# Moving two of each step's score-maximum chunks into the score tile, in a four-layer attention and FFN kernel

## Chip, core and metric

The kernel runs on one core of one Trainium2 chip. The metric is the device time of one execution in microseconds. Three runs of the kernel before gave 11,102.46, 11,116.24 and 11,129.85 us, a median of 11,116.24.

## The reference

A batch of 16 sequences x of 256 tokens and 128 channels goes through four layers. Each layer adds an attention result and then a feed-forward result (experts, convolution or plain) to x. Every layer has a cross attention of 16 heads over a context of 1,601 positions with 64 channels. In layers l0, l1 and l3 a head has 8 channels, in l2 it has 32; l0 and l2 also attend over the 256 tokens themselves. The part that the change touches is the softmax of the cross attention:

```
scores = jnp.einsum('bhqd,bhkd->bhqk', qh, kh) * scale
attn = jax.nn.softmax(scores, axis=-1)
out = jnp.einsum('bhqk,bhkd->bhqd', attn, vh)
```

The softmax is taken with its row maximum subtracted, so for each head and each of the 256 queries the kernel needs the largest of 1,601 scores before it can form the first exponential.

## The kernel before

**Slabs and steps.** The cross attention of one sequence in one layer is cut into four slabs of four heads; 16 sequences, four layers and four slabs make 256 slabs, two sequences being in flight. The heads of a slab stand in four groups of 32 partitions. For the 8-channel heads the 32 rows hold high and low parts of queries and keys, in a rounded fp32 format (`spread`, L407 ff.); in l2 they hold 32 channels in fp32. A slab's main loop has seven steps (`Slab.steps`, L530): six take two key tiles of 128, the last takes the remaining 65 keys.

**One step of the main loop** (L1169 to L1192) issues, in this order:

1. `maxima(part - 3)`: some chunks of the *next* slab's row maxima;
2. `st_ops` (L447): the scores of this slab, transposed, keys on partitions. Two score tiles of two PSUM banks each, `sc[0]` for heads 0 and 1, `sc[1]` for heads 2 and 3. The products go key tile by key tile over the four heads, and then one product per head adds the negated row maximum (`nmT`);
3. `exps` (L462): one ScalarE exponential for each score tile, PSUM to SBUF;
4. `maxima(part)`: three more chunks of the next slab;
5. `weigh_back` (L1132): the value products of the *previous* step, accumulated in one PSUM bank `av` that is held over the slab (in l2 also products with ones, for the sums);
6. two or three calls of `slot` (L1073), which advance all side work by one piece each: keys, values and contexts of later slabs, the layers' projections, norms and feed-forward parts.

Under the manual schedule each engine executes its instructions in this written order, so an instruction that waits holds up all that is behind it on its engine.

**Maxima chunks.** A slab needs 32 of them: two query halves q, four chunks c of about 400 keys, four heads g, queued in `self.todo` with g innermost (L537 ff.). `Slab.maxima` (L544) takes the first of the queue: one product of 128 queries by 400 keys into a PSUM bank (`bank`, tile group `pb`, four banks), and one VectorE `tensor_reduce` (L552) of this bank into `mx[:, q, g, c]`. Two closures are returned; the loop helper `maxima(want)` issues the products at once and the reductions after them. With `part = 32 * (j + 1) // 6` the six full steps take 5, 5, 6, 5, 5 and 6 chunks, three of them after the scores. In the seventh step `thirds` (L556) reduces `mx` to the negated maximum (L558), GpSimd splits it into three bf16 parts, and `shift` transposes them to `nmT` for the next slab.

**PSUM.** Eight banks: tile group `ps` has two score tiles of two banks (tag `st`), group `pb` four single banks. One of these holds `av`; the other three serve the maxima chunks and all side work. The tiles of the self attention (`own_attention`, L564, in slots of l0 and l2) use the two score tiles too.

Of the kernel before, what the change touches and what calls it, by code (L numbers as in the profile page):

```python
# [11 lines left out]
F32 = mybir.dt.float32  # L12
# [4 lines left out]
ALU = mybir.AluOpType  # L17
AX = mybir.AxisListType
PSUM = bass.MemoryType.PSUM

P = 128
T = 256
# [32 lines left out]
def rows_of(kt):  # L55
    return min(P, NK - kt * P)
# [18 lines left out]
def model(ctx: ExitStack, tc: tile.TileContext, d, out):  # L75
    nc = tc.nc
# [78 lines left out]
    ps = ctx.enter_context(tc.tile_pool(name="ps", bufs=2, space=PSUM))  # L155
# [4 lines left out]
    def name(base):  # L160
        uid[0] += 1
        return f"{base}_{uid[0]}"

    def bank():
        return pb.tile([P, 512], F32, tag="bank", name=name("bank"))
# [5 lines left out]
    def mm(o, l, r, start=True, stop=True, free=False):  # L171
        nc.tensor.matmul(out=o, lhsT=l, rhs=r, start=start, stop=stop, skip_group_check=free)  # L172
# [6 lines left out]
    with setup as sp:  # L179
# [24 lines left out]
        p = bank()  # L204
# [11 lines left out]
        p = bank()  # L216
# [230 lines left out]
    def st_ops(att, s, t0, n, r, nmT, pairs=(0, 1)):  # L447


        sc = {hp: ps.tile([P, 2, 2, T], F32, tag="st", name=name("st")) for hp in pairs}  # L450
        heads = [g for hp in pairs for g in (2 * hp, 2 * hp + 1)]
        for i in range(n):
            k0 = (t0 + i) * P
            for g in heads:
                h = slice(32 * g, 32 * g + 32)
                mm(sc[g // 2][:r, g % 2, i, :], att.k[s][h, k0 : k0 + r], att.q[h, s, :], i == 0, False)
        for g in heads:
            h = slice(32 * g, 32 * g + 32)
            mm(sc[g // 2][:r, g % 2, :n, :], ones16[h, :r], nmT[h, :].unsqueeze(1).broadcast_to([32, n, T]), False, True)
        return [sc[hp] for hp in pairs]  # L460

    def exps(att, sc, n, r):  # L462
        e = probs()
        nc.scalar.activation(e[:r, :, :n, :], sc[:r, :, :n, :], AF.Exp, scale=att.scale)  # L464
        return e

    def zeroed(att):
        a = bank().rearrange("p (u q) -> p u q", u=2)
        n = 1 if att.d8 else 2
        mm(a[:, :n, :], zero16[:, :P], zero16.unsqueeze(1).broadcast_to([1, n, T]), True, False, True)  # L470
        return a

    def weigh(att, s, av, pr, t0, n, r, last, heads=range(4), sums=True, values=True):
        for i in range(n):
            fin = last and i == n - 1
            if values:
                for g in heads:
                    m = 9 if att.d8 else 32
                    mm(av[32 * g : 32 * g + m, 0, :], att.value(s, t0 + i, g, r), pr[g // 2][:r, g % 2, i, :],
                       False, fin, True)  # L480
            if sums and not att.d8:
                for g in heads:
                    mm(av[32 * g : 32 * g + 32, 1, :], ones[:r, :32], pr[g // 2][:r, g % 2, i, :], False, fin, True)
# [21 lines left out]
    def thirds(n, nm):  # L505

        r = sm.tile([P, 2, 4], F32, tag="third", name=name("third"))
        a, b, c = (n[:, :, i::32] for i in range(3))
        nc.gpsimd.tensor_copy(a, nm)  # L509
        nc.gpsimd.tensor_tensor(r, nm, a, ALU.subtract)  # L510
        nc.gpsimd.tensor_copy(b, r)
        nc.gpsimd.tensor_tensor(c, r, b, ALU.subtract)
# [14 lines left out]
    class Slab:  # L527


        steps = [(t, min(2, NT - t), rows_of(t)) for t in range(0, NT, 2)]  # L530
# [13 lines left out]
        def maxima(self):  # L544

            g, q, c, k0, k1 = self.todo.popleft()
            att, s = self.att, self.s
            p = bank()
            h = slice(32 * g, 32 * g + 32)

            def reduce():
                nc.vector.tensor_reduce(self.mx[:, q, g, c : c + 1], p[:, : k1 - k0], AX.X, ALU.max)  # L552

            return lambda: mm(p[:, : k1 - k0], att.q[h, s, q * P : (q + 1) * P], att.k[s][h, k0:k1]), reduce

        def thirds(self):  # L556
            nm = sm.tile([P, 2, 4], F32, tag="nm", name=name("nm"))
# [498 lines left out]
    def advance(g):  # L1056
        try:
            return True, next(g)
        except StopIteration:
            return False, None  # L1060
# [12 lines left out]
    def slot():  # L1073
        begin()
        if later:
            g = later.popleft()
            if advance(g)[0]:
                later.appendleft(g)
        for i, l in enumerate(lines):
            if i == turn[0] % 2:  # L1080
                advance(l)
        turn[0] += 1
        for c in list(chains):
            if c[0] is not None and c[0] in ready:
                if not ready[c[0]].done:
                    continue
                del ready[c[0]]
            alive, att = advance(c[1])
            if att is not None:
                ready[c[0]] = att  # L1090
            if not alive:
                chains.remove(c)

    def until(cond):
        for _ in range(2000):
            if cond():
                return
            slot()
        raise RuntimeError("the slots do not come to an end")
# [3 lines left out]
    def slab(i):  # L1103

        n, s = divmod(i, 4)
        if n >= len(seq):
            return None
        b = seq[n][0]
        until(lambda: b in ready and not ready[b].done and n in k_of and s in k_of[n])
        att = ready[b]  # L1110
        att.k, att.v = k_of[n], v_of.setdefault(n, {})
        slabs_of[i] = Slab(att, s, i % 2)
        return slabs_of[i]

    def finish(sl, i):

        yield from normalised(sl.att, sl.s, sl.av)
        if sl.s == 3:
            sl.att.done = True
        if not sl.att.d8 or sl.s == 3:  # L1120
            vp_room.give()

    with tc.manual_schedule():
        sl = slab(0)
        while sl.todo:
            for o in sl.maxima():
                o()
        sl.thirds()
        sl.shift()
        back = None  # L1130

        def weigh_back():  # L1132

            nonlocal back
            if back is None:
                return
            sl, i, j, pr = back
            n = i // 4
            t0, m, r = sl.steps[j]
            if j == 0:  # L1140
                until(lambda: (0 if sl.att.d8 else sl.s) in v_of.get(n, {}))
                sl.att.v = v_of[n]
                sl.av = zeroed(sl.att)
            last = j == len(sl.steps) - 1
            weigh(sl.att, sl.s, sl.av, pr, t0, m, r, last)
            back = None
            if last:
                g = finish(sl, i)
                if advance(g)[0]:
                    later.append(g)  # L1150

        for i in range(4 * len(seq)):
            nxt = slab(i + 1)
            steps = sl.steps
            emitted = 0

            def maxima(want):

                nonlocal emitted
                ops = []  # L1160
                while nxt is not None and emitted < want:
                    a, c = nxt.maxima()
                    a()
                    ops.append(c)
                    emitted += 1
                for c in ops:
                    c()

            for j, (t0, m, r) in enumerate(steps):  # L1169

                part = 32 * (j + 1) // (len(steps) - 1)
                if j < len(steps) - 1:
                    maxima(part - 3)
                elif nxt is not None:
                    nxt.thirds()
                sc = st_ops(sl.att, sl.s, t0, m, r, sl.nmT)
                pr = [exps(sl.att, t, m, r) for t in sc]
                if j < len(steps) - 1:
                    maxima(part)
                weigh_back()  # L1180
                back = (sl, i, j, pr)
                if j == len(steps) - 1 and nxt is not None:
                    nxt.shift()
                slot()
                slot()

                if i // 4 + 1 < len(seq) and seq[i // 4 + 1][1] == "l2":
                    slot()
            kp_room.give()
            sl = nxt  # L1190
        weigh_back()
        until(lambda: not chains and not later)  # L1192
# [119 lines left out]
```

## Time and profile before

| | |
|---|---|
| median of three runs | 11,116.24 us |
| the profiled execution's time | 11,069.08 us |
| its span, first to last instruction | 11,067.1 us |
| mean granted TensorE clock | 0.815 of full speed |
| TensorE products busy | 9,761.1 us (88%) |
| VectorE busy | 5,929.3 us (54%) |
| ScalarE busy | 4,978.5 us (45%) |
| single maxima, L552 | 8,192, 4,155.2 us busy |
| exponentials, L464 | 3,840, 3,500.5 us busy |
| chunk products (`bank<-k,q`) | 3,573.1 us busy |

PE is TensorE's products, PEld its weight loads, DVE VectorE, ACT ScalarE, POOL GpSimd, SP the queue that issues most transfers. Busy times of a group are the union of its instructions, so pipelined instructions count once; the mean of one is its own latency. All TensorE products are recorded by one helper, L172, and are told apart by the tiles they write and read: `bank<-k,q` a maxima chunk, `st<-q,k` a score product, `bank<-p,v` a value product. An fp32 product stands in the trace twice. A group's line ends with its engine's idle time just before it and with what ended that idle time.

### The profile page before, as it was taken

The page shows a single profiled execution, that of the slowest core. Times are in us where ns is not written, and L with a number is a line of the kernel's source. Part 1 is how long each engine was busy: PE and PEld are TensorE (multiplying, and loading weights), DVE is VectorE, ACT ScalarE, POOL GpSimd, SP SyncE. Part 2 cuts the span into 40 slices and gives each one's busy share as a digit, 9 for nine tenths or more (in the row PEclk, how much of TensorE's full clock was granted, in tenths as well). Part 3 has the DMA queues.
Part 4 walks back from the last instruction along what each step waited for, and adds up shares of the span by engine and source line. Part 5 has one row for each costly group of instructions (what it writes and reads, how often), then busy time and mean ns, then how long its engine had stood idle before and what let it go on. Part 6 is the DMA issues. An engine that isn't in the chain of part 4 may idle for free.

```text
span 11067.1 us, 204917 instructions
## 1 busy us (share of the span) xinstructions
PE 9761.1 (88%) x86834; PEld 5294.4 (48%) x86874; DVE 5929.3 (54%) x13070; ACT 4978.5 (45%) x6812; POOL 952.3 (9%) x2283
## 2 busy tenths in 40 slices
PE   6989899897998979889798897998979889898898
PEld 3445444454444544445454454444545445444454
DVE  5545555455554555545455454554555545465455
ACT  3544455444553445434454344543445434454444
POOL 2000100001000010000100001000010000100000
PEclk8779777797878978789777897778977789687898
DMA  2100111001110011100111001110011100111011
GB/s 58 37 7 15 36 45 37 7 16 39 42 37 7 19 38 42 34 7 19 38 44 32 7 19 42 40 32 7 19 38 43 33 7 19 38 44 32 7 24 27
DMA packets 158828, 313.10 MB, mean 28 GB/s; under 512 B 65163, under 2 KB 116275, under 8 KB 157910
## 3 DMA queue, kind: packets, MB, share of 16 engines
q1 hardware_dynamic: 154676, 297.83, 11.7%
q8 instruction: 683, 11.19, 0.4%
q14 instruction: 235, 1.93, 0.1%
q0 software_dynamic: 768, 1.48, 0.0%
q10 hardware_dynamic: 2466, 0.68, 0.0%
HBM read 98.31 MB, written 2.10 MB: 9 GB/s over the span
## 4 chain that ended last, share of the span: by engine, by line
PE 71%; DVE 14%; ACT 5%; issue 4%; POOL 3%; SPq 2%; DMA 1%; another core or an unknown queue 0%; DVEq 0%; POOLq 0%; ACTq 0%
PE bank L172 57%; PE st L172 10%; DVE mx L552 5%; ACT p L464 3%; DVE nm L579 2%; SPq L411 2%; PE mx L172 1%; PE bank L492 1%; POOL p L603 1%; PE bank L298 1%; DVE z L282 1%; POOL rs L278 1%; DVE st L275 1%; DVE hl L405 1%; ACT y L239 1%
## 5 line engine op out<-in xcount | busy, mean ns | idle before, releaser
L552 DVE TENSOR_REDUCE mx<-bank 128x1 f32<-128x400 f32 (+2 forms) x8192 | 4155.2, 567 | 2296.9 <-PE bank L172 2271.8
L464 ACT ACTIVATE p<-st 128x1024 f32<-128x1024 f32 (+1 forms) x3840 | 3500.5, 963 | 3568.3 <-PE st L172 2358.6
L172 PE MATMUL bank<-k,q 32*128 32x400 f32 (+2 forms) x10240 | 3573.1, 557 | 495.3 <-DVE mx L552 261.3
L172 PEld LDWEIGHTS bank<-k,q 32*128 32x128 f32 x10240 | 1600.6, 211 | 1928.7 <-DVE mx L552 1111.4
L172 PE MATMUL bank<-p,v 128*9 128x256 f32 (+3 forms) x27648 | 2412.4, 460 | 12.6 <-POOL p L603 12.6
L172 PE MATMUL st<-q,k 32*128 32x256 f32 (+1 forms) x18176 | 1974.8, 391 | 126.2 <-DVE nm L579 69.2
L172 PEld LDWEIGHTS st<-q,k 32*128 32x128 f32 (+1 forms) x18176 | 1300.8, 210 | 443.7 <-ACT p L464 140.4
L172 PE MATMUL st<-nmT,ones 32*128 32x512 bf16 (+1 forms) x7680 | 1270.1, 435 | 0.0
L172 PEld LDWEIGHTS bank<-p,v 128*9 128x9 f32 (+3 forms) x27648 | 676.3, 104 | 1175.4 <-issue 922.6
L172 PE MATMUL bank<-p,ones 128*32 128x256 f32 (+1 forms) x7680 | 607.1, 389 | 18.1 <-ACT p L464 18.1
L509 POOL CAST nmp<-nm 128x8 bf16<-128x8 f32 x384 | 83.6, 218 | 5441.9 <-DVE nm L558 3668.7
L278 POOL TENSOR_TENSOR rs<-rs,neghalf 128x2 f32<-128x2 f32 x240 | 167.5, 698 | 3491.1 <-DVE rs L277 3491.1
L172 PEld LDWEIGHTS <-ones 32*128 32x128 bf16 (+1 forms) x7680 | 408.1, 108 | 39.4
L579 DVE TENSOR_REDUCE nm<-mx 128x4 f32<-128x1024 f32 x256 | 301.8, 1221 | 215.3 <-PE mx L172 210.6
L239 ACT COPY v<-bank 128x512 f32<-128x512 f32 (+3 forms) x592 | 228.6, 448 | 328.8 <-PE bank L172 328.8
L172 PEld LDWEIGHTS bank<-p,ones 128*32 128x32 f32 (+1 forms) x7680 | 250.8, 113 | 216.6 <-ACT p L464 43.6
L502 DVE RECIPROCAL rc<-bank 128x256 f32<-128x256 f32 x128 | 224.9, 1757 | 193.6 <-PE bank L172 189.3
L603 POOL TENSOR_SCALAR_AFFINE_SELECT p<-p 128x1024 f32<-128x1024 f32 x256 | 266.6, 1063 | 653.3 <-PE bank L172 352.7
L464 ACT ACT_TABLE_LOAD x141 | 180.9, 1283 | 312.9 <-PE st L172 201.9
L172 PE MATMUL bank<-ws,h 128*128 128x128 f32 x1664 | 297.9, 343 | 3.2 <-DVE h L1027 0.8
L768 DVE TENSOR_TENSOR x<-bank,x 128x256 f32<-128x256 f32 x144 | 61.1, 425 | 446.0 <-PE bank L172 446.0
L172 PEld LDWEIGHTS bank<-ws,h 128*128 128x128 f32 x1664 | 267.2, 248 | 39.0 <-DVE mx L552 13.6
(240 smaller groups left out, 7274.4 us busy)
## 6 DMA issues: line engine op xcount, KB each, us to landing
k<-hl SPq DMA_DIRECT2D x768, 200.2 KB, 4.0
q<-hl SPq DMA_DIRECT2D x1024, 32.0 KB, 1.9
ws<-in_s_l_a_li_dram SPq DMA_DIRECT2D x32, 768.0 KB, 4.3
ws<-in_s_l3f_dram SPq DMA_DIRECT2D x32, 768.0 KB, 6.7
ws<-in_s_l0f_dram SPq DMA_DIRECT2D x32, 512.0 KB, 5.6
ws<-in_s_l_a_qkv_dram SPq DMA_DIRECT2D x16, 768.0 KB
k<-hl SPq DMA_DIRECT2D x256, 32.0 KB, 1.9
ws<-in_s_l3f_dram SPq DMA_DIRECT2D x16, 384.0 KB
```

The costliest lines, as they stand in the source:

```text
L172: nc.tensor.matmul(out=o, lhsT=l, rhs=r, start=start, stop=stop, skip_group_check=free)
L239: nc.scalar.copy(o, i)
L275: nc.vector.bn_stats(out=st[:, q, :], in_=src[:, q, :])
L278: nc.gpsimd.tensor_tensor(rs, rs, neghalf[:, 0:2], ALU.pow)
L282: nc.vector.tensor_scalar(z[:, q, :], src[:, q, :], mv[:, q, 0:1], rs[:, q : q + 1], ALU.subtract, ALU.mult)
L298: nc.tensor.transpose(p[:, q * P : (q + 1) * P], z[:, q, :], ident)
L411: nc.sync.dma_start(out=raw(o)[r::4, :], in_=raw(hl[c])[32 * s : 32 * s + 32, :])
L464: nc.scalar.activation(e[:r, :, :n, :], sc[:r, :, :n, :], AF.Exp, scale=att.scale)
L502: nc.vector.reciprocal(rc, av[:, 1, :])
L552: nc.vector.tensor_reduce(self.mx[:, q, g, c : c + 1], p[:, : k1 - k0], AX.X, ALU.max)
L579: nc.vector.tensor_reduce(o, sc[hp], AX.X, ALU.max, negate=True)
L603: nc.gpsimd.affine_select(out=e, in_=e, pattern=[[0, 2], [sign * P, 2], [-sign, T]], compare_op=op, fill=0.0, base=0, channel_multiplier=sign,
```

## The change

A new method takes two chunks from the other end of the queue (the last of the list: two neighbouring heads of one q and c), writes their products into the two banks of a *score tile* (group `ps`, tag `st`) instead of two single banks, and reduces both with one instruction of 128 x 2 x 400 elements, whose output is two elements per partition. It is called once in each of the six full steps, after the value products of `weigh_back` and before the slots. The tile that is free first at this point is the one that the step's first exponential reads. The other 20 chunks are taken as before, in the new shares 3, 3, 4, 3, 3 and 4 per step, of which two (not three) stand after the scores.

```diff
+        def maxima2(self):
+
+            q, c, k0, k1 = self.todo.pop()[1:]
+            g0 = self.todo.pop()[0]
+            p = ps.tile([P, 2, 2 * T], F32, tag="st", name=name("mx2"))
+            for g in (g0, g0 + 1):
+                h = slice(32 * g, 32 * g + 32)
+                mm(p[:, g - g0, : k1 - k0], self.att.q[h, self.s, q * P : (q + 1) * P], self.att.k[self.s][h, k0:k1])
+            nc.vector.tensor_reduce(self.mx[:, q, g0 : g0 + 2, c], p[:, :, : k1 - k0], AX.X, ALU.max)
...
-                part = 32 * (j + 1) // (len(steps) - 1)
+
+                part = (32 - 2 * (len(steps) - 1)) * (j + 1) // (len(steps) - 1)
                 if j < len(steps) - 1:
-                    maxima(part - 3)
+                    maxima(part - 2)
                 elif nxt is not None:
                     nxt.thirds()
                 sc = st_ops(sl.att, sl.s, t0, m, r, sl.nmT)
...
                 back = (sl, i, j, pr)
+                if j < len(steps) - 1 and nxt is not None:
+                    nxt.maxima2()
                 if j == len(steps) - 1 and nxt is not None:
                     nxt.shift()
                 slot()
```

## The prediction

> **What bounds the kernel now.** I read the page first (busy shares, chain of waits, costliest groups), then the table of waits, then the timeline.
>
> ```profile
> PE 9761.1 (88%) x86834; PEld 5294.4 (48%) x86874; DVE 5929.3 (54%) x13070; ACT 4978.5 (45%) x6812; POOL 952.3 (9%) x2283
> ...
> PE 71%; DVE 14%; ACT 5%; issue 4%; POOL 3%; SPq 2%; DMA 1%; another core or an unknown queue 0%; DVEq 0%; POOLq 0%; ACTq 0%
> ...
> L552 DVE TENSOR_REDUCE mx<-bank 128x1 f32<-128x400 f32 (+2 forms) x8192 | 4155.2, 567 | 2296.9 <-PE bank L172 2271.8
> L172 PEld LDWEIGHTS bank<-k,q 32*128 32x128 f32 x10240 | 1600.6, 211 | 1928.7 <-DVE mx L552 1111.4
> L579 DVE TENSOR_REDUCE nm<-mx 128x4 f32<-128x1024 f32 x256 | 301.8, 1221 | 215.3 <-PE mx L172 210.6
> ```
>
> PE carries the chain. VectorE is half idle, and yet the weight loads of the chunk products wait 1,111 us for its maxima. The table of waits says the same:
>
> ```profile
> PEld bank L172 <- DVE mx L552: 1304.6, 3116, 5.7
> PEld st L172 <- ACT p L464: 140.4, 215, 1.8
> ```
>
> Score tiles hardly wait for the exponentials (140 us); banks wait for maxima. Where that sits is seen in a step that has nothing else on PE (timeline; start, length, engine):
>
> ```profile
> 3011.38 0.45 PE L172 MATMUL bank<-k,q 32*128 32x400 f32 x2
> 3011.38 0.56 PE L172 MATMUL st<-q,k 32*128 32x256 f32 x6
> ...
> 3011.86 2.50 DVE L552 TENSOR_REDUCE mx<-bank 128x1 f32<-128x400 f32 x5 [0.98 <-PE bank L172]
> ...
> 3012.39 1.94 ACT L464 ACTIVATE p<-st 128x1024 f32<-128x1024 f32 x2 [1.13 <-PE bank L172]
> 3012.49 0.18 PEld L172 LDWEIGHTS bank<-k,q 32*128 32x128 f32 x1 [0.49 <-DVE mx L552]
> ...
> 3013.34 1.05 PE L172 MATMUL bank<-p,v 128*9 128x256 f32 x16
> ```
>
> Two chunk products, the scores, a third chunk; then all three free banks are full (the fourth holds the running sum), and chunks four and five go at VectorE's 0.5 us rhythm. The value products start 1.96 us after the scores. And a step with other work:
>
> ```profile
> 3030.87 0.56 PE L172 MATMUL st<-q,k 32*128 32x256 f32 x7
> ...
> 3031.53 0.60 DVE L282 TENSOR_SCALAR z<-x,mv,rs 128x128 f32<-128x128 f32 x2 [0.82 <-POOL rs L278]
> 3031.88 1.94 ACT L464 ACTIVATE p<-st 128x1024 f32<-128x1024 f32 x2 [1.07 <-PE st L172]
> 3032.05 2.97 DVE L552 TENSOR_REDUCE mx<-bank 128x1 f32<-128x400 f32 x6
> 3032.68 1.41 PE L172 MATMUL bank<-k,q 32*128 32x400 f32 x3 [0.90 <-DVE mx L552]
> ...
> 3034.01 1.05 PE L172 MATMUL bank<-p,v 128*9 128x256 f32 x16
> ```
>
> A layer norm holds VectorE, so all six maxima come late and the value products start 3.14 us after the scores.
>
> **What the Trainium skill says.** "Perfetto Trace Analysis", Identifying Performance Opportunities: the same gap repeating on the engine that should be saturated can mean too little PSUM for the next tile. The trace agrees (0.3 to 0.5 us at each late chunk). "VectorE: DVE Perf Modes", The perf-mode tier table: a reduction runs at 1x only, so width costs in full. It agrees: (1221-567) ns for 624 more elements is 1.05 ns each. "TensorE: Matmul & The Clock Gate", Part 1: TensorE runs at half clock unless recent windows were busy. It agrees: the mean grant is 0.815, and a chunk product takes 0.41 us in some steps and 0.70 in others.
>
> **The steps counted.** I cut the timeline at each step's first chunk product (steps j = 0 to 4 of each slab, 1,275 in all; times 6/5 for j = 5) and sorted by the length from the last value product to the next chunk product; under 0.7 us I call a step bare. "Period" is first exponential to first exponential; "b-w" first score product to first value product.
> - bare, 8-wide heads, full clock: 172 (206 scaled), period 3.17, b-w 2.24
> - bare, 8-wide, half clock: 145 (174), 4.37, 2.34
> - bare, layer l2: 104 (125), 4.62, 2.87
> - with side work: full clock 388 (466), b-w 2.16; half 250 (300), 2.92; l2 216 (259), 3.20
>
> **Part 1, chunks taken out of the b-w stretch.** 3 or 4 bank chunks remain of 5 or 6 in each of six steps, with two after the scores instead of three. With three banks free nothing waits for a maximum of its own step. What remains of b-w at full clock: the scores' products (0.75 us at 3014.42) plus the last chunk's 0.37 to the value products, about 1.15 us (the step at 3024.99, whose chunks did not wait, took 1.21 to the clearing product ahead of its value products). At half clock 1.5, by the same sum from 3007.65; in l2, where each score product stands twice in the trace, 2.1 (2.10 from the first score to the first exponential). So PE saves 1.0, 1.4 and 1.1 us, less the moved pair's own products: 0.1 (two row groups side by side; three in a row start within 0.1 at 3014.33), 0.2 and 0.3.
>
> **Part 2, the pair's wait for the first exponential.** It ends 1.97 us after the scores start (1.01 + 0.97 in the bare step), while value products that start at 1.15 are through at 2.1; at half clock 2.64 against 3.3, in l2 3.07 against 4.0. Hidden by the value products: 0. Where a table load or an evacuation delays the exponential, PE and all side work behind it wait; in PE's queue these are the two slots' products.
>
> **Part 3, one reduction for two chunks.** No row has 800 elements; between the rows for 400 and 1024: 567 + 400 x 1.05 = 0.98 us. Bounds: 0.92 (two at the 0.507 spacing of 4155.2/8192, one fixed part less) to 1.2 (the 1024 row). VectorE's total falls by at most 0.1 x 1,530 = 150 us; it is 54% busy, so nothing. Behind it stand the slots' VectorE operations. Today their place is behind the last maximum, which ends 3.0 to 3.4 us after the scores start (14.36 in the bare step); in the new order the pair ends at 3.6. These 0.2 to 0.6 us are taken off what passes to the next step, below.
>
> **Part 4, the score tile held.** This is the new wait. The next step's first two heads take the second exponential's tile; heads three and four need the pair's. In a bare step at full clock: pair products at b+2.1, first maximum 0.48 later (the 3011.38 row to the 3011.86 row), 0.98 for the reduction, 0.04 to PE: b+3.6. From there 0.9 to the next exponential (1.01, less the two products already made): b+4.5, a period of 3.5 against 3.17. Half clock: 3.3+0.74+0.98+0.04+1.45-1.67 = 4.84 against 4.37. l2: 4.0+0.97+0.98+0.04+1.9-2.1 = 5.8 at most, 5.7 taken, against 4.62. Loss: 206 x 0.33 + 174 x 0.47 + 125 x 1.08 = 68+82+135 = **+285 us**. With over about 1.5 us of side work on PE this wait is covered.
>
> **The sum.** Side-work steps could save 466 x 0.9 + 300 x 1.2 + 259 x 0.8 = 419+360+207 = 986 us if all of it reached the next step. It doesn't: in two thirds of them PE already waits over 0.3 us inside the slots for ScalarE or VectorE (transposes that wait for an evacuation, products that wait for a layer norm), and these engines are no earlier, since the second exponential still ends 2.94 us after the scores start. I let a third pass in full and a quarter of the rest: 0.34 + 0.66/4 = 0.5, so 493 us. Bounds: 0.15 (only where PE never waits, less what banks take) to 0.8. Net 285-493 = -208, about **-200 us**. The profiled execution spans 11,067.1 us and took 11,069.08, so 10,869; it is 47 us under the median 11,116.24 of the three runs, on which the forecast is 10,916.
>
> No DMA is moved. The last step's pair delays the slab's negated maximum (L558), but the score tile that the next step needs is freed by the same reduction, so the shift is no later against the scores.
>
> **Rivals.**
> - *The score tile becomes the bound (slower).* Place: third and fourth head of each next step's scores. For it: bare steps are a third of all, and the side-work slots are short in many others (1.3 us typical for one class in each layer). Against it: VectorE is free when the pair arrives. It decides once less than 285/986 = 0.29 of the saving passes. At 0.1: +285-99 = +186, 11,302 us. TensorE at half clock more often, because it waits more, pulls the same way.
> - *All passes (much faster).* In the layer-norm step above, the late maxima cost two steps' worth, which my sum doesn't credit. At 0.95: 285-937 = -652, 10,464 us. Against it: PE's waits for ScalarE in the slots.
> - *Cancelled.* 0.29 passes: about 11,116.
> - *It doesn't do what it says:* the pair may be given the second exponential's tile. It would then wait until b+3.0, nearly 1 us more in every step; I count it with the slower case.
>
> **Chances.** Forecast case, -35 to -480 us: 0.42. All passes: 0.12. Within 0.3% (33 us; about what a measurement can tell from no change): 0.10. Slower: 0.36. So faster 0.54. Range: 0.8 passing gives -504; 0.15 gives +137: 10,612 to 11,253, taken as 10,620 to 11,250, with about one in ten left out at each end.
>
> **What would show it.** Right: the waits of PE for L552's single maxima fall from 1,566 us (1304.6 + 261.3) below 500; b-w near 1.2 in full-clock steps; a new wait "PE st <- DVE mx2" of 300 to 800 us, in bare steps; bare periods of 3.5, 4.8 and 5.7; VectorE busy within 3% of before. Wrong: that wait over 1,000 us, or spread over steps with side work; the pair's products waiting over 300 us for the exponential; a mean grant below 0.79.

## The result, and the profile after

The changed kernel is slower: 11,542.98 us (median of four runs, 11,527.76 to 11,566.57) against 11,109.35 us for the kernel before in the same session. The ratio is 1.0398, with a 95% interval of 1.0361 to 1.0434. The profiled execution spans 11,546.1 us, 479 us more than before; the mean granted clock is 0.808 instead of 0.815. The forecast was 10,916 us, and its range ended at 11,250.

The page of the changed kernel, the rows that answer to those shown of before (L589 is the old L579; L564 is the pair's reduction; `mx<-k,q` holds the pair's products, and those of the self attention):

```profile
PE 9745.0 (84%) x86834; PEld 5211.1 (45%) x86874; DVE 5955.1 (52%) x11540; ACT 4976.8 (43%) x6812; POOL 953.2 (8%) x2283
...
PE 69%; DVE 16%; ACT 6%; issue 4%; POOL 2%; SPq 2%; DMA 1%; ACTq 0%; POOLq 0%; DVEq 0%
...
L552 DVE TENSOR_REDUCE mx<-bank 128x1 f32<-128x400 f32 (+2 forms) x5132 | 2713.2, 569 | 1944.3 <-PE bank L172 1911.0
...
L564 DVE TENSOR_REDUCE mx<-mx 128x2 f32<-128x800 f32 (+1 forms) x1530 | 1517.8, 992 | 1618.3 <-PE mx L172 1434.4
...
L172 PEld LDWEIGHTS bank<-k,q 32*128 32x128 f32 x6412 | 1007.9, 219 | 765.7 <-issue 215.4
...
L589 DVE TENSOR_REDUCE nm<-mx 128x4 f32<-128x1024 f32 x256 | 301.7, 1221 | 176.7 <-PE mx L172 172.0
```

TensorE is busy as long as before (9,745 against 9,761 us), so the whole growth of the span lies in PE's idle time: 1,801 us instead of 1,306. VectorE's time is as before too. The reduction of 800 elements takes 992 ns; I had 980. The weight loads of single chunks hardly wait for maxima any more. The waits of the changed kernel show what came instead:

```profile
PEld mx L172 <- ACT p L464: 895.9, 1253, 2.1
...
PEld st L172 <- DVE mx L564: 549.0, 635, 1.6
...
PE st L172 <- DVE mx L564: 331.7, 596, 1.3
...
PEld st L172 <- ACT p L464: 267.8, 347, 1.8
...
PEld bank L172 <- DVE mx L552: 177.3, 320, 3.2
...
PE st L172 <- ACT p L464: 160.3, 340, 1.6
PE mx L172 <- ACT p L464: 158.8, 253, 1.6
```

Scores wait for the pair's reduction and for the second exponential, and the pair waits for the first exponential. (The 896 us of the weight loads include the value products' own time, during which PE is not idle; PE's idle share is the 159.) A bare step of the changed kernel, at half clock, from one row of value products to the next:

```profile
3131.52 1.90 PE L172 MATMUL bank<-p,v 128*9 128x256 f32 x16
...
3133.35 0.70 PE L172 MATMUL mx<-k,q 32*128 32x400 f32 x2
...
3133.86 0.41 PE L172 MATMUL st<-q,k 32*128 32x256 f32 x2
3134.09 0.99 DVE L564 TENSOR_REDUCE mx<-mx 128x2 f32<-128x800 f32 x1 [1.41 <-PE bank L172]
...
3135.14 0.80 PE L172 MATMUL st<-q,k 32*128 32x256 f32 x6 [0.87 <-DVE mx L564]
...
3136.28 1.94 ACT L464 ACTIVATE p<-st 128x1024 f32<-128x1024 f32 x2 [3.19 <-PE st L172]
3136.65 0.13 PEld L172 LDWEIGHTS bank<-p,v 128*9 128x9 f32 x8 [0.56 <-issue]
```

The order is serial: value products (1.83 us), pair to VectorE (0.74), reduction and handover (1.05), and then six of eight score products, two chunks and the next value products (1.51 from 3135.14), 5.13 us in all. VectorE has nothing to do from 3132.68 to 3134.09, while the value products run. And the layer-norm step, again at half clock:

```profile
3158.49 0.91 PE L172 MATMUL st<-q,k 32*128 32x256 f32 x7
...
3160.54 1.90 PE L172 MATMUL bank<-p,v 128*9 128x256 f32 x16
...
3162.36 0.70 PE L172 MATMUL mx<-k,q 32*128 32x400 f32 x2
3162.99 0.29 PEld L298 LDWEIGHTS bank<-ident,z 128*128 128x128 f32 x2 [0.34 <-issue]
```

Scores to value products fell from 3.14 us (at full clock) to 2.05, as meant. But the pair stands alone between value products and a transpose, both of which use all 128 rows of the array: 0.63 us pass before the transpose starts. Over the trace the median from the pair to the next slot product is 0.38 us at full clock, 0.63 at half clock and 0.87 behind fp32 pairs.

### The profile page after: what moved, and what is told of

Read it like the earlier page. It is cut to its first block, busy times and chain, and to the rows that moved or that the text cites. A ratio compares the mean times of both kernels' runs of the same rounds, so it can differ in the third digit from the quotient of the medians.

```text
span 11546.1 us, 203244 instructions
## 1 busy us (share of the span) xinstructions
PE 9745.0 (84%) x86834; PEld 5211.1 (45%) x86874; DVE 5955.1 (52%) x11540; ACT 4976.8 (43%) x6812; POOL 953.2 (8%) x2283
## 3 DMA queue, kind: packets, MB, share of 16 engines
q14 instruction: 224, 1.83, 0.1%
## 4 chain that ended last, share of the span: by engine, by line
PE 69%; DVE 16%; ACT 6%; issue 4%; POOL 2%; SPq 2%; DMA 1%; ACTq 0%; POOLq 0%; DVEq 0%
PE bank L172 46%; PE st L172 13%; PE mx L172 8%; DVE mx L564 6%; ACT p L464 4%; DVE nm L589 2%; SPq L411 2%; DVE mx L552 1%; PE bank L492 1%; PE bank L298 1%; DVE z L282 1%; DVE rc L502 1%; POOL p L613 1%; POOL rs L278 1%; DVE st L275 1%
## 5 line engine op out<-in xcount | busy, mean ns | idle before, releaser
L552 DVE TENSOR_REDUCE mx<-bank 128x1 f32<-128x400 f32 (+2 forms) x5132 | 2713.2, 569 | 1944.3 <-PE bank L172 1911.0
L172 PE MATMUL st<-q,k 32*128 32x256 f32 (+1 forms) x18176 | 2189.1, 409 | 549.1 <-DVE mx L564 331.7
L172 PE MATMUL bank<-k,q 32*128 32x400 f32 (+2 forms) x6412 | 2394.1, 576 | 228.4 <-DVE mx L552 79.8
L564 DVE TENSOR_REDUCE mx<-mx 128x2 f32<-128x800 f32 (+1 forms) x1530 | 1517.8, 992 | 1618.3 <-PE mx L172 1434.4
L172 PEld LDWEIGHTS st<-q,k 32*128 32x128 f32 (+1 forms) x18176 | 1383.0, 213 | 1077.1 <-DVE mx L564 549.0
L172 PE MATMUL mx<-k,q 32*128 32x256 f32 (+2 forms) x5364 | 1194.4, 536 | 264.8 <-ACT p L464 158.8
L172 PEld LDWEIGHTS bank<-k,q 32*128 32x128 f32 x6412 | 1007.9, 219 | 765.7 <-issue 215.4
L172 PE MATMUL st<-nmT,ones 32*128 32x512 bf16 (+1 forms) x7680 | 1305.5, 439 | 0.0
L172 PEld LDWEIGHTS mx<-k,q 32*128 32x128 f32 x5364 | 490.2, 219 | 1228.1 <-ACT p L464 895.9
L172 PE MATMUL bank<-p,ones 128*32 128x256 f32 (+1 forms) x7680 | 651.1, 410 | 17.8 <-ACT p L464 17.8
L589 DVE TENSOR_REDUCE nm<-mx 128x4 f32<-128x1024 f32 x256 | 301.7, 1221 | 176.7 <-PE mx L172 172.0
L613 POOL TENSOR_SCALAR_AFFINE_SELECT p<-p 128x1024 f32<-128x1024 f32 x256 | 266.6, 1063 | 748.6 <-PE bank L172 435.9
```

Of the source, the lines that this page charges most:

```text
L564: nc.vector.tensor_reduce(self.mx[:, q, g0 : g0 + 2, c], p[:, :, : k1 - k0], AX.X, ALU.max)
L589: nc.vector.tensor_reduce(o, sc[hp], AX.X, ALU.max, negate=True)
L613: nc.gpsimd.affine_select(out=e, in_=e, pattern=[[0, 2], [sign * P, 2], [-sign, T]], compare_op=op, fill=0.0, base=0, channel_multiplier=sign,
```

## The experiments

The times of before in the four sessions were 11,091, 11,095, 11,085 and 11,105 us.

### The shorter stretch alone, and the pair's products alone

```diff
-            nc.vector.tensor_reduce(nm, self.mx, AX.X, ALU.max, negate=True)
+            nc.vector.tensor_reduce(nm, self.mx[:, :, :, 0:1], AX.X, ALU.max, negate=True)
...
-                if j < len(steps) - 1 and nxt is not None:
-                    nxt.maxima2()
```

> The twelve chunks of each slab that go into the score tile are left out altogether (their products and their reduction), and the row maximum that is subtracted is that of the first key chunk alone. This is the saving of the shorter stretch between scores and value products by itself, with no pair anywhere. If half of what that stretch saves reaches the next step, as forecast, plus the bare steps' own saving (about 430 us: 0.7 us in 206 full-clock steps, 1.0 in 174 at half clock, 0.9 in 125 of l2): about 10,190 us. If the slots' waits for ScalarE and VectorE eat the saving (the rival): 10,700 us or more.

Measured: 9,750.77 us, 0.8787 of before (0.8760 to 0.8814). The twelve chunks cost 1,340 us where they stood before the change. My full saving was 986 us in the steps with side work, from which the pair's own products were already taken off; without them, as in this run, it is 1,171 us (466 x 1.0 + 300 x 1.4 + 259 x 1.1), and 1,601 with the 430 of the bare steps. Of this, 84% came. The rival falls, and so does my "half". The slots' waits do eat a part: PE's wait for an evacuation (ScalarE's copy out of PSUM) ahead of a transpose rises from 144 us to 296, as this row of the run shows.

```profile
PE bank L492 <- ACT y L239: 295.9, 201, 2.4
```

One thing more changed that I had no term for. The mean granted clock is 0.854 in this run and 0.815 before; of the value products of 8-wide heads 27% take the longer time of the half clock instead of 44%. So the 1,340 us hold both the shorter stretch and a faster clock, and no run takes them apart.

The second run keeps the pair's products and drops its reduction (`tensor_reduce` goes out of `maxima2`; the change to `thirds`, the first two lines of the diff above, stays in all runs that take the row maximum of the first chunk):

> As the changed kernel, but nobody reads the pair: its products are made in the score tile, its reduction is left out (and the row maximum is that of the first chunk, as in the run with the chunks left out). Theory 1, the score tile is the loss (scores of heads three and four wait for the pair's reduction): nearly all of the difference between the changed kernel and the run with the chunks left out goes, at most 150 us over that run. Theory 2, the pair's products are the loss in PE's queue (they wait for the first exponential, and what is behind them waits until they are through, 0.38, 0.63 or 0.87 us): 500 us or more over that run.

Measured: 10,367.01 us (0.9336; 0.9303 to 0.9369), 616 us over the run without the pair and 1,176 under the changed kernel. Both theories hold in part: the products alone cost 616 us, and two thirds of the pair's price comes with its reduction. Here too the clock moves along: of the 1,184 us between the two profiles 470 are idle time of PE, and in the other 714 PE counts as busy with the same 86,834 products, at a mean grant of 0.808 instead of 0.848. Whether the waits slow the clock or something else does is not shown.

### What of the reduction costs: VectorE's time, the handover or the hold

```diff
-            nc.vector.tensor_reduce(self.mx[:, q, g0 : g0 + 2, c], p[:, :, : k1 - k0], AX.X, ALU.max)
+            nc.vector.tensor_reduce(self.mx[:, q, g0 : g0 + 2, c], convw[:, 0:2, : k1 - k0], AX.X, ALU.max)
```

> As the run without the reduction, but VectorE does in the same place one reduction of the same 2 x 400 elements of a constant in SBUF, so that its time is spent and the score tile is not held (the row maximum is that of the first chunk). If the held score tile costs: at most 300 us over the 10,370 us of the run without the reduction. If VectorE's 0.98 us ahead of the slots' own VectorE work costs: 800 us or more over it.

Measured: 10,623.95 us (0.9567; 0.9541 to 0.9592), 257 over the run without the reduction. VectorE's time is not free, as I had it. But this run does not give its price in the changed kernel, since its reduction waits for no product and can run while VectorE would be idle, beside the value products:

```profile
2891.82 1.90 PE L172 MATMUL bank<-p,v 128*9 128x256 f32 x16
...
2892.57 0.98 DVE L564 TENSOR_REDUCE mx<-convw 128x2 f32<-128x800 f32 x1
...
2893.65 0.70 PE L172 MATMUL mx<-k,q 32*128 32x400 f32 x2
```

It starts 0.29 us ahead of the pair's first product in the median (ahead of it in 1,063 of 1,530 pairs); in the changed kernel it starts 0.74 us behind it. In the next two runs the operand is `p[:, :, 0:1]` and `p[:, :, 0:200]`:

> As the changed kernel, but the reduction of the pair reads one element of each of its two banks instead of 400 (the row maximum is that of the first chunk). The score tile is held until VectorE has come to it, but VectorE spends hardly any time on it. If the length of the reduction is what holds the scores up: 10,450 to 10,750 us. If the handover itself costs (the pair's products end, VectorE is reached in its order, PE is told): 11,000 us or more.

> The changed kernel with the pair's reduction over 200 of the 400 columns of each bank (row maximum of the first chunk); 0.57 us instead of 0.99. The short hold gave 10,724 us and the whole one 11,543. If each microsecond of the hold costs the same from the first on, 11,100 to 11,200 us; if there is slack that covers the first half, as I forecast for steps with side work, below 11,000 us.

Measured: 10,724.15 us (0.9668; 0.9650 to 0.9687) and 11,012.73 us (0.9940; 0.9919 to 0.9960). The pair's reduction in these two profiles:

```profile
L564 DVE TENSOR_REDUCE mx<-mx 128x2 f32<-128x2 f32 x1530 | 245.9, 161 | 1553.6 <-PE mx L172 1373.5
```

```profile
L564 DVE TENSOR_REDUCE mx<-mx 128x2 f32<-128x400 f32 x1530 | 879.5, 575 | 1561.6 <-PE mx L172 1377.9
```

So a reduction that ends almost at once costs 357 us over none. Lengthening it from 161 to 575 ns adds 289, and from 575 to 992 ns 530: the price per unit rises. The half run came in under "each microsecond costs the same" and above "slack covers the first half", so neither expectation was met. What PE's scores themselves wait for the reduction is this, for one and for 200 columns of each bank; for all 400 it is the 331.7 us shown above:

```profile
PE st L172 <- DVE mx L564: 0.5, 1, 0.5
```

```profile
PE st L172 <- DVE mx L564: 106.5, 262, 0.9
```

With one element the scores hardly wait for it (0.5 us), and still the run loses 357. There VectorE is held: it sits idle for 1,374 us until the pair's products are made, and the slots' VectorE operations stand behind. So neither the 257 us nor the 357 us is the price of one cause alone, and no run has them apart; the held score tile accounts directly for 332 us of PE's idle time in the changed kernel.

### The place or the tile

The two chunks stay behind the value products, but go into single banks:

```diff
-            p = ps.tile([P, 2, 2 * T], F32, tag="st", name=name("mx2"))
+            p = [bank(), bank()]
...
+            for g in (g0, g0 + 1):
+                nc.vector.tensor_reduce(self.mx[:, q, g, c : c + 1], p[g - g0][:, : k1 - k0], AX.X, ALU.max)
```

> The changed kernel with one part undone: the two chunks stay behind the value products, but go into two single banks with two single reductions, as all other chunks do. The score tile is held by nobody. If holding the score tile is what costs (1,176 us from the run without the reduction to the changed kernel): between the run without the reduction, 10,370 us, and about 10,800 us, faster than both kernels. If it is VectorE's time in its own order, or the products' place in PE's queue: 11,300 us or more.

Measured: 11,497.45 us (1.0357; 1.0332 to 1.0382), 45 us from the changed kernel. I had expected this to beat both. That the *score* tile is held can't be what decides: two held single banks are as bad. Here the products that need a bank wait, most of them single chunks of the next step:

```profile
PE bank L172 <- DVE mx L552: 191.9, 183, 4.8
...
PE bank L172 <- DVE mx L565: 136.6, 253, 0.7
```

(L565 is the pair's two reductions; in the changed kernel the wait for L552 is 86 us.) The same run without the two reductions:

> The run with the two chunks in single banks behind the value products, their two reductions left out (row maximum of the first chunk). These products wait for no exponential and hold nothing for VectorE. Against the run without the reduction (10,370 us, products in the score tile) it tells the two parts of the 616 us apart. If these are mainly the wait for the first exponential and the tile: 9,850 to 10,050 us. If they are mainly the products themselves, standing alone in PE's queue between products that use all rows: 10,250 us or more.

Measured: 10,261.31 us (0.9262; 0.9246 to 0.9278). The products alone therefore cost 510 us over no pair even where they wait for no exponential (some 50 us of it are waits for banks: PE waits 135 us for single maxima here and 83 in the run without the reduction); the score tile and its exponential add 106. And the two reductions cost 1,236 us here, against 1,176 in the score tile. So the price goes with the place behind the value products and not with the tile. How much of it is a held bank and how much the place in VectorE's order these two runs don't tell, since both have both. In the next run the pair stands between the first two slots:

> The changed kernel with the pair between the two slots instead of ahead of both, so that the first slot's products cover the wait for the first exponential. If that wait and what it delays in the first slot are a main part: 11,250 to 11,400 us. If the hold of the score tile is: the pair comes later, less covers its reduction, and the time is that of the changed kernel or more, 11,540 to 11,800 us.

Here the call of `maxima2` stands between the first two calls of `slot`. Measured: 11,694.72 us (1.0552; 1.0528 to 1.0575), 152 over the changed kernel, as expected from the hold: less work is left to cover the reduction. The wait of the scores for it rises from 332 to 787 us:

```profile
PE st L172 <- DVE mx L564: 787.2, 964, 8.5
PEld mx L172 <- ACT p L464: 474.1, 663, 3.6
```

The pair *ahead* of the value products, whose 1 to 2 us would then cover its reduction, can't be had in this form: the first exponential, for whose tile the pair waits, may itself wait for a probability tile that these value products free. It was not tried.

### Where the pair stands in the slab

```diff
+                both = nxt is not None and sl.att.d8 and nxt.att.d8
+                part = (20 if both else 32) * (j + 1) // (len(steps) - 1)
...
+                if j < len(steps) - 1 and both:
```

> The pair only where this slab and the next both have 8-wide heads; all other slabs as before the change. By layer the changed kernel lost 377 us in l2, 89 in l3, 28 in l0 and won 17 in l1. If the loss belongs to l2's long fp32 products: about 11,200 us. If it is spread, and l2 only shows what was put off to it: 11,350 us or more.

Measured: 11,164.72 us (1.0075; 1.0047 to 1.0103). Most of the loss is l2's. The next run takes the pair out of the sixth step instead (`part = (3, 6, 10, 13, 16, 22, 22)[j]`, three chunks behind the scores there):

> No pair in the sixth step (there six single chunks, three after the scores, as before the change); pairs in the other five. Between the sixth step's exponentials and the next slab's first ones the changed kernel lost 314 of 477 us. If that is the sixth step's own (the short seventh step behind it cannot cover the pair): about 11,230 us. If it is the price of the last pair, wherever it stands: 11,450 us or more.

Measured: 11,353.75 us (1.0236; 1.0203 to 1.0268); 189 us of the sixth step's 314 come back. Both together:

> The pair in steps one to five only, and only where this slab and the next have 8-wide heads. By the timeline these steps won about 100 us in the changed kernel, and the others lost all of it. If the pair's gain and loss belong to the step where it stands: 10,980 to 11,050 us, faster than before. If what one step wins is lost at the next wait: 11,090 us or more.

Measured: 11,121.58 us (1.0033; 1.0021 to 1.0045). What the timeline showed as 100 us won by steps is not there: most of what one step wins is lost further on. The sixth steps, which hold no pair here, are 0.6 us longer than before in 8-wide heads. No kernel that computes the whole row maximum beat the kernel before.

### The order of the single chunks, without any pair

In the kernel before, `maxima(part - 3)` becomes `part - 2`, `part - 4` and `part - 6` (none ahead of the scores):

> The kernel before, with one of the three chunks that stand after the scores moved ahead of them (two after, as in the changed kernel), all 32 in single banks. If three free banks and VectorE's 0.5 us rhythm set the stretch, whatever the order: within 0.3% of before. If the place of the chunks alone shortens it: 10,900 us or less.

> The kernel before with one chunk fewer ahead of the scores and one more behind them (1 or 2 ahead, 4 behind), all in single banks. Moving one the other way cost 2.2%. If a chunk ahead of the scores costs because scores and exponentials start later, with the same stretch to the value products: 10,850 to 11,000 us, faster than before, and part of what the changed kernel won came from this, not from the pair. If the three banks alone set it: within 0.3% of before.

> The kernel before with all 5 or 6 chunks behind the scores. By the same reading the scores start earliest, but three banks stand empty while they run, and VectorE starts its row of maxima 0.5 us later: 11,000 to 11,200 us. If an early start of the scores outweighs that: below 10,900 us.

Measured: 11,325.18 us (1.0221; 1.0206 to 1.0237), 11,540.81 us (1.0394; 1.0378 to 1.0409) and 12,618.02 us (1.1363; 1.1343 to 1.1383). All three expectations of a gain, or of no change, fell. With one chunk more ahead, PE's idle time until a single maximum has freed a bank rises from 261 us to 430; with one more behind the scores it rises to 502, with the value products waiting behind it. Of the run with four behind, the weight loads:

```profile
PEld bank L172 <- DVE mx L552: 1674.3, 3382, 5.7
```

That is 1,674 us against 1,305 before. Of the four orders tried, three behind the scores is the fastest. These runs keep all 32 chunks in the steps, so they don't tell what the changed kernel's own order (one fewer ahead and one fewer behind) is worth; they give no sign that its order alone wins anything.

## Why the prediction was wrong, by its own steps

I cut four of the other traces like that of before, by the same 1,529 steps and their classes in the kernel *before*. Mean period in us; the sixth step's reaches over the seventh to the next slab. "12 chunks left out" is the first run, "+ products" the run without the reduction, "+ short reduction" the one that reduces one element of each bank:

| class, number | before | 12 chunks left out | + products | + short reduction | changed |
|---|---|---|---|---|---|
| bare, 8-wide, 317 | 3.72 | 2.96 | 3.27 | 3.44 | 4.12 |
| bare, l2, 104 | 4.62 | 4.08 | 4.64 | 4.96 | 5.96 |
| side work, 8-wide, 638 | 7.83 | 6.82 | 7.10 | 7.18 | 7.47 |
| side work, l2, 216 | 9.20 | 8.18 | 8.69 | 9.31 | 9.79 |
| sixth, 8-wide, 190 | 8.44 | 7.84 | 8.42 | 8.62 | 9.51 |
| sixth, l2, 64 | 10.02 | 9.27 | 10.27 | 10.97 | 11.74 |

**Part 1, the saving: right in direction, "half" was too little.** Side-work steps without the pair save 1.01 and 1.02 us each, (1.01 x 638 + 1.02 x 216) x 6/5 = 1,038 us, nine tenths of the 1,171 that I had for them without the pair's products. But it is not quite the saving that I had described. The stretch from scores to value products shrank by 0.76 us (8-wide) and 0.66 (l2) in these steps; at full clock it is 1.43 us, not my 1.15. The rest of the 1.01 us lies outside it, where one chunk fewer stands ahead of the scores and the clock is faster.

**Part 2, the pair in PE's queue: wrong.** I took 0.1 to 0.3 us for its products and nothing for its wait. The products cost 0.28 us in 8-wide steps with side work, 0.51 in l2, and 0.58 and 1.00 in the sixth. I read the price from chunk products that stand next to score products, where all use 32 rows and start within 0.1 us; behind value products and ahead of slot products the next product starts 0.38 to 0.87 us later. The exponential's part is small: 159 us of PE's idle time, and 106 us in the run that avoids it.

**Part 3, VectorE's time: wrong.** "It is 54% busy, so nothing" cost 257 us even where the reduction could run ahead of the pair. A share of busy time says nothing of the slots' operations that stand behind the pair in VectorE's order: PE's idle time before the transposes and products that need a layer norm's z rose from 59 us (54 in the run without the reduction) to 151, as this row of the changed kernel shows:

```profile
PE bank L298 <- DVE z L282: 151.1, 68, 11.8
```

**Part 4, the score tile held: right for bare steps; for the rest the pair's price is the term that failed.** Bare: I forecast 3.5 and 4.84 us at the two clocks, weighted 4.11; measured 4.12. That they agree to 0.01 is luck: sorted by their clock in the changed kernel it is 3.64 and 4.89, with more steps at full clock than before. In l2 5.7; measured 5.96. I wrote that with over 1.5 us of side work the wait of the scores is covered, and it is: of PE's 332 us, 195 follow bare steps, 108 sixth steps and 29 steps with side work. But I let that stand for the whole price of the reduction there. From the run without the reduction to the changed kernel, steps *with* side work lost 0.37 us (8-wide) and 1.10 us (l2), and the sixth steps 1.09 and 1.47. That PE waits longer for z, and equally long where no score tile is held (152 us with single banks), speaks for VectorE's order, and the slower clock is in it; the shares are not separated.

The pair's whole price, from the first run to the changed kernel, is 1,792 us, and the table gives its place: 563 us in bare steps, 763 in steps with side work, 475 in sixth steps. By my terms these were about 597, 154 and 150 (my bare loss of 285 us was net of the 430 saved there; the 6/5 is taken out here). So my price was close in bare steps and over 900 us too low in steps with side work and sixth steps, and the saving of 1,340 us fell short of what the pair cost.

**The sixth step was folded into the sum with 6/5: wrong.** I argued that its pair delays nothing. It is followed by a step of half the scores and no chunks, and its period grew most: +1.07 and +1.72 us per slab, 314 of the 477 us that the cut steps lost. Side-work steps ended 104 us better instead of 411 (493 without the 6/5), and bare ones 267 us worse (238 forecast). These three differences make up the 685 us between my -208 and the +477.

**The rivals.** The slower one named the right wait and the right side, but its mechanism was too narrow: it let the saving fail to pass (0.1 of it), when nine tenths passed and the pair gave back more. It gave 11,302 us. Nearly all my signs misled. The waits for single maxima fell from 1,566 us to 263, the scores' wait for the pair was 332 us and mostly in bare steps, the pair's products waited 159 us, VectorE and the grant stayed inside what I had called right, and the kernel was slower. Only the stretch from scores to value products told: at full clock it was 1.47 us in steps with side work and 1.87 in bare ones, not near 1.2. The wait at one place was no test of a price that is paid behind it.

**What stays open.** Why steps of l2 with side work lose three times as much to the reduction as 8-wide ones was not separated. Their pair needs 0.99 us to reach VectorE, not 0.49 or 0.74, which may be part of it. How much of each run's time is the granted clock, and what moves the clock, is open too. That the value products are the natural cover for maxima is argued, not shown: VectorE idles during them in the changed kernel, two chunks behind them cost 403 us more in single banks than in the old order (11,497 against 11,095), but the reverse order was not tried.

## What to carry to other kernels

Work that leaves a bottleneck's queue is priced by a run without it, and its new place by what stands on both sides of it there: the same short-row products cost little next to others of their kind and 0.38 to 0.87 us between full-row and slot products. A consumer that frees a shared buffer probably belongs ahead of the long operation that needs no buffer; that it lost by being moved behind it is measured here, that the cover is the reason is argued. A mean busy share of an engine does not say that an added operation is free, when operations that others wait for stand behind it in its order. And a test run that keeps an operation but drops what it waits for may let it run earlier: look in its trace where it went.

## What the runs showed that I had not expected

- Two products of 32 rows x 400 columns behind value products of 128 rows held the next slot product off by 0.38 us at full clock, 0.63 at half clock and 0.87 in fp32 (medians). Where a single chunk's product followed instead, it started 0.01 us after the pair in 125 of 220 cases at full clock, and 0.28 to 0.34 us after it in the others.
- One chunk more or fewer behind the scores moves this kernel by 2.2 to 3.9%, and all of them behind by 13.6%, with the mean granted clock falling from 0.815 to 0.753. The grant does not simply follow PE's idle share: 12% idle goes with 0.815 (before), 15% with 0.854 (chunks left out), 16% with 0.808 (changed) and 15% with 0.753 (all behind the scores).
- The width of a reduction costs in full, as the Trainium skill has it ("VectorE: DVE Perf Modes", The perf-mode tier table: a reduction runs at 1x only), over two banks too: 161, 575 and 992 ns for 2, 400 and 800 elements, 1.04 ns for each more.
